# A graph network's prologue: the first block's rows gathered from x and normalised edge by edge

## The chip, the cores and the metric

The kernel runs on one core of one Trainium2 chip. The metric is the device time of one execution in microseconds; the kernel before took 6227.5 us, the median of three runs (6223.47, 6227.50 and 6228.35). A profile is one further execution of the same program under the hardware profiler; its own time is given beside it below.

The engines are named as the profile names them: PE (matrix products), DVE (vector engine), ACT (scalar engine), POOL (GpSimd), SP (the engine whose queue issues most transfers). Each engine works through its own instructions in order and waits for the others through semaphores.

## The reference

6250 nodes with 128 values each, 200000 edges sorted by their receiving node. Two layers, each added to x.

```python
h = jnp.maximum(_layernorm(x, axis=-1), 0.0)
x = x + L0(h, src, dst, W, attn_l, attn_r, bias)      # attention over edges
h = jnp.maximum(_layernorm(x, axis=-1), 0.0)
x = x + L1(h, edge_attr_4, edge_attr_8, ..., stack([src, dst]))

# L0
z = (feat @ W).reshape(N, HEADS, PER_HEAD)
el = jnp.einsum('nhp,hp->nh', z, attn_l)
er = jnp.einsum('nhp,hp->nh', z, attn_r)
e = jax.nn.leaky_relu(el[src] + er[dst], negative_slope=0.2)
a = jnp.exp(e - segment_max(e, dst)[dst])
out = segment_sum(z[src] * a[:, :, None], dst) / segment_sum(a, dst) + bias
```

Layer 1 runs a small network over each edge's attributes, multiplies the sender's row with its weights and sums the messages by receiver. For this change only the beginning matters: z and el of every node, er of every node, and the row (z, el) of the sender of every edge.

## The kernel before

The edges lie in 1563 tiles of 128 (one edge per partition), 16 tiles (KB) to a block: 98 blocks. A block's receivers fall into a window of nodes, so that sums over receivers are products with one-hot matrices on PE. Rows of senders are fetched from a table in DRAM: t0 (136 values: z and el) for layer 0, t1 and t1z (128 values) for layer 1.

*Prologue* (lines 842 to 957). The 50 tiles of x come in ten loads on SP's queue (line 865; the groups gx have 2, 3, 5, then 6 tiles, the last 4). Behind them on the same queue stand the index list src_col, the receivers twice (d_i, and q_i shifted by one edge) and a small off. A loop over k runs four stages of different groups side by side: statistics of group k on DVE (moments), the square root of group k-1 on ACT (deviation), the normalisation of group k-2, dealt out to ACT, POOL and DVE by tile number (lines 892 to 900), and for group k-3 the transposes and products on PE, with the ReLU (line 911) and the copies to zt on ACT, for the last two groups on DVE. zt goes to the table t0 on SP's queue; POOL copies its last eight columns to er_all. PE, DVE and ACT keep the order in which the code is written (manual_schedule); POOL and SP are ordered by the scheduler of the language.

Behind the loop POOL gathers the 16 tiles of block 0 from t0 into z_first (line 930). A gather is one indirect transfer of 128 rows, issued by POOL:

```python
nc.gpsimd.indirect_dma_start(
    out=to[:, k, :width], out_offset=None, in_=table,
    in_offset=bass.IndirectOffsetOnAxis(ap=src_col[:, t : t + 1], axis=0))
```

Meanwhile DVE tests whether the edges are as the fast path needs them (lines 932 to 950: is any receiver smaller than the one before, does a tile leave its window), writes the count to ok_i, and splits er_all into three bf16 parts er3 (lines 952 to 957). All engines read ok_i and branch (line 959) into even_edges.

*even_edges* (line 965). It opens the pools const, then z_pool (five row buffers of 16 x 136 values, tile g), then others; a pool takes the next free addresses, so that z_pool lies above the constants, which lie where the prologue's tiles were. SP loads the constants and, in the pool build, the receivers once more (d_i, q_i, nxt_i), from which DVE and ACT make masks. Then the loop of layer 0 over the blocks (line 1363): take_rows(g + 3) issues a later block's gathers on POOL, and the steps for blocks g-2 to g+2 are woven together on PE, DVE and ACT. One tile in every third block is fetched row by row on SP's queue instead (rows_by_row). Layer 1 (line 1488) has a loop of the same kind, with z_first used again for its first block.

Of the kernel before, what the change touches and what calls it, by code (L numbers as in the profile page):

```python
# [9 lines left out]
F32 = mybir.dt.float32  # L10
BF = mybir.dt.bfloat16
I32 = mybir.dt.int32
AF = mybir.ActivationFunctionType
OP = mybir.AluOpType
AX = mybir.AxisListType
# [3 lines left out]
P = 128  # L19
H = 8  # L20
D = 16
F = H * D
ZW = F + H
# [6 lines left out]
KB = 16  # L30
# [711 lines left out]
def tile_even_edges(  # L742
# [46 lines left out]
    def to_table(table, of, i, n, eng):  # L789

        if i == 0:
            eng.dma_start(table[: P - W0, :], of[W0:, 0, :])
            if n > 1:
                to = table[P - W0 : n * P - W0]
                eng.dma_start(to.rearrange("(j p) f -> p j f", p=P), of[:, 1:n, :])
            return
        to = table[i * P - W0 : (i + n) * P - W0]
        eng.dma_start(to.rearrange("(j p) f -> p j f", p=P), of[:, :n, :])
# [20 lines left out]
    def deviation(pool, mv, n, name, m=P):  # L819
        rs = pool.tile([P, n, 1], F32, name=f"rs{name}")  # L820
        nc.scalar.activation(rs[:m], mv[:m, :, 1:2], AF.Sqrt, bias=eps[:m])
        return rs

    def normal(pool, mv, rs, n, name, m=P):

        nc.vector.reciprocal(rs[:m], rs[:m])
        mr = pool.tile([P, n, 1], F32, name=f"mr{name}")
        nc.vector.scalar_tensor_tensor(mr[:m], mv[:m, :, 0:1], -1.0, rs[:m], op0=OP.mult, op1=OP.mult)
        return rs, mr
# [8 lines left out]
    def tiles_of(a, first):  # L838
        return a[first : first + TG * P * P].rearrange("(g t e) -> t g e", t=P, e=P)


    with tc.manual_schedule(engines={mybir.EngineType.PE, mybir.EngineType.DVE,
                                     mybir.EngineType.Activation}), \
# [11 lines left out]
        nc.scalar.sqrt(root, eps)  # L855
        w_ext = fx.tile([P, CW], F32, name="fw_ext")
# [9 lines left out]
        nc.sync.dma_start(src_col, srcc)  # L866
        d_i = fx.tile([P, TG, P], I32, name="fd_i")
        nc.sync.dma_start(d_i, tiles_of(dstt, P))
        q_i = fx.tile([P, TG, P], I32, name="fq_i")
        nc.sync.dma_start(q_i, tiles_of(dstt, P - 1))  # L870
        off = fx.tile([P, TG], F32, name="foff")
        nc.sync.dma_start(off, nums[:, NB * KB : NB * KB + TG])
# [7 lines left out]
        er_all = fx.tile([P, NX, H], F32, name="fer_all")  # L880
        NC = len(gx)
        mvs, rss, mrs, hs = {}, {}, {}, {}
        todo, done, outs = [], [], []
        for k in range(NC + 3):
            if 0 <= k - 1 < NC:
                rss[k - 1] = deviation(fp, mvs[k - 1], gx[k - 1][1], f"x{gx[k - 1][0]}")
            c = k - 2
            if 0 <= c < NC:
                i, n = gx[c]
                rs, mr = rss[c], mrs[c] = normal(fp, mvs[c], rss[c], n, f"x{i}")  # L890
                h = hs[c] = fp.tile([P, 10, P], F32, name="fh")
                for j in range(n):
                    by = (i + j) % 7
                    if by in ((2, 6) if c < NC - 2 else (2,)):
                        nc.scalar.activation(h[:, j, :], xs[c][:, j, :], AF.Identity,
                                             bias=mr[:, j, :], scale=rs[:, j, :])
                    else:
                        eng = nc.gpsimd if by in (0, 3, 5) and c < NC - 2 else nc.vector
                        eng.tensor_scalar(h[:, j, :], xs[c][:, j, :], mvs[c][:, j, 0:1],
                                          rs[:, j, :], op0=OP.subtract, op1=OP.mult)  # L900
            if k >= 3:
                i, n = gx[k - 3]
                zt = fp.tile([P, 10, CW], F32, name="zt")
                todo += [(k - 3, zt, j0, min(3, n - j0)) for j0 in range(0, n, 3)]
            while todo:
                c, zt, j0, m = todo.pop(0)
                p_t = fp_ps.tile([P, 4, P], F32, name="p_t")
                for j in range(m):
                    nc.tensor.transpose(p_t[:, j, :], hs[c][:, j0 + j, :], ident)
                h_t = fp.tile([P, 3, P], F32, name="h_t")  # L910
                nc.scalar.activation(h_t[:, :m], p_t[:, :m], AF.Relu)
                done.append((c, zt, j0, m, h_t))
                while len(done) > (1 if k < NC + 2 or todo else 0):
                    c, zt, j0, m, h_t = done.pop(0)
                    p_z = fp_ps.tile([P, 3, CW], F32, name="p_z")
                    for j in range(m):
                        nc.tensor.matmul(p_z[:, j, :], h_t[:, j, :], w_ext, start=True, stop=True)
                    outs.append((c, zt, j0, m, p_z))
                    while len(outs) > (1 if k < NC + 2 or todo or done else 0):
                        c, zt, j0, m, p_z = outs.pop(0)  # L920
                        copy = nc.scalar.copy if c < NC - 2 else nc.vector.tensor_copy
                        copy(zt[:, j0 : j0 + m, :], p_z[:, :m])
                        i, n = gx[c]
                        if j0 + m == n:
                            to_table(t0, zt[:, :, :ZW], i, n, nc.sync)
                            nc.gpsimd.tensor_copy(er_all[:, i : i + n, :], zt[:, :n, ZW:])
            if k < NC:
                i, n = gx[k]
                mvs[k] = moments(fp, xs[k], n, f"x{i}")
        gather(z_first, t0, range(KB), ZW)  # L930

        bad = fx.tile([P, TG, P], F32, name="fbad")
        nc.vector.tensor_tensor(bad, d_i, q_i, OP.is_lt)
        vs = fx.tile([P, 4], F32, name="fvs")
        nc.vector.tensor_reduce(vs[:, 0:1], bad.rearrange("p g e -> p (g e)"), AX.X, OP.add)
        w3 = fx.tile([P, 3, TG], F32, name="fw3")
        ef = fx.tile([P, 2, TG], F32, name="fef")
        nc.vector.tensor_sub(ef[:, 0, :], d_i[:, :, 0], off)
        nc.vector.tensor_sub(ef[:, 1, :], d_i[:, :, P - 1], off)
        nc.vector.tensor_single_scalar(w3[:, 0, :], ef[:, 0, :], 0.0, op=OP.is_lt)  # L940
        nc.vector.tensor_single_scalar(w3[:, 1, :], ef[:, 1, :], float(P), op=OP.is_ge)
        nc.vector.tensor_tensor(w3[:, 2, :], ef[:, 0, :], ef[:, 1, :], OP.is_equal)
        nc.vector.tensor_reduce(vs[:, 1:2], w3.rearrange("p a g -> p (a g)"), AX.X, OP.add)
        ones = fx.tile([P, 1], F32, name="fones")
        nc.vector.memset(ones, 1.0)
        p_v = fp_ps.tile([P, 4, P], F32, name="p_t")
        nc.tensor.matmul(p_v[:1, 0, :2], ones, vs[:, :2], start=True, stop=True)
        vr = fx.tile([1, 1], F32, name="fvr")
        nc.vector.tensor_reduce(vr, p_v[:1, 0, :2], AX.X, OP.add)
        nc.vector.tensor_copy(ok_i, vr)  # L950
# [14 lines left out]
def even_edges(tc, v):  # L965
# [5 lines left out]
    xp, dstc, y4, f8, bias, out, moments, deviation, normal, gather, tiles_of = (v[k] for k in (  # L971
        "xp", "dstc", "y4", "f8", "bias", "out", "moments", "deviation", "normal", "gather", "tiles_of"))
    with ExitStack() as ctx:
        const = ctx.enter_context(tc.tile_pool(name="fconst", bufs=1))
        z_pool = ctx.enter_context(tc.tile_pool(name="fz", bufs=5))
# [22 lines left out]
        wup = const.tile([P, P], F32, name="fwup")  # L998
        nc.sync.dma_start(wup, v["wup"])
        a1p = const.tile([P, KB // 2, P], F32, name="fa1p")  # L1000
        nc.sync.dma_start(a1p, v["a1p"])
        a2p = const.tile([P, P], F32, name="fa2p")
        nc.sync.dma_start(a2p, v["a2p"])
        a3p = const.tile([P, 2, P], F32, name="fa3p")
        nc.sync.dma_start(a3p, v["a3p"])
        b1 = const.tile([P, 1], F32, name="fb1")
        nc.sync.dma_start(b1, v["b1"])
        b2 = const.tile([P, 1], F32, name="fb2")
        nc.sync.dma_start(b2, v["b2"])
        wout = const.tile([P, 2, P], F32, name="fwout")  # L1010
        nc.sync.dma_start(wout, v["wout"])
# [11 lines left out]
        with tc.tile_pool(name="fbuild", bufs=1) as build:  # L1023
            d_c = build.tile([P, TU], I32, name="fd_c")
            nc.sync.dma_start(d_c, dstc)
            d_i = build.tile([P, TG, P], I32, name="fd_i")
            nc.sync.dma_start(d_i, tiles_of(dstt, P))
            q_i = build.tile([P, TG, P], I32, name="fq_i")
            nc.sync.dma_start(q_i, tiles_of(dstt, P - 1))
# [20 lines left out]
            nc.sync.dma_start(t1z[LATE * P - W0 :].rearrange("(j p) f -> p j f", p=P), zeros)  # L1050

# [796 lines left out]
```

## Time and profile before

| | |
|---|---|
| median of the runs | 6227.5 us |
| the profiled execution's own time | 3888.67 us |
| its span, first to last instruction | 3886.9 us |
| granted TensorE clock, mean | 0.803 |
| first gather of block 0 starts | 42.58 us |
| first gather of block 1 starts | 63.16 us |
| last gather starts | 3870.95 us |
| busy between 42.58 and 63.16: POOL, DVE, PE | 15.70, 5.34, 0.69 us |
| DMA share and GB/s, 0 to 42.58 us | 0.79, 220 |
| DMA share and GB/s, 63 to 1950 us | 0.28, 64 |

The profile is one execution; its durations are sums and means of that one. It was 2339 us shorter than the runs, and it holds nothing of the runs themselves. A line of a group gives: code line, engine, operation, output <- inputs by the program's names, count, then busy time, mean ns of one, idle time of the engine just before them and what ended most of it. "issue" is time in which the engine waited for nothing that the profile shows.

### The profile page before, as it was taken

To read this page: it belongs to the slowest core of one execution; us is meant where nothing else is said; L and a number is where in the kernel's file an instruction comes from. 1 tells how busy PE (TensorE), PEld (TensorE's weight loads), DVE (VectorE), ACT (ScalarE), POOL (GpSimd) and SP (SyncE) were. 2 spreads that over 40 slices of the span, in tenths; PEclk is the share of its full clock that TensorE was granted. 3 is DMA by queue.
4 is the path that set the end of the run, shared out by engine and by line. 5 is a ranking of instruction groups with operands and counts; after the bars stand their busy time and mean duration, and the time that the engine had idled before them with its cause. 6 is when DMAs were issued, how large, how long until landed. Compare 5 with 4: busy or idle time off the path is not lost. (4 is left out here: it accounts for less than half of the span.)

```text
span 3886.9 us, 62701 instructions
## 1 busy us (share of the span) xinstructions
PE 2848.8 (73%) x14785; PEld 2401.2 (62%) x14785; DVE 2224.5 (57%) x5408; ACT 1396.8 (36%) x3612; POOL 2913.0 (75%) x3096
## 2 busy tenths in 40 slices
PE   3766666666666766666678888888877777778777
PEld 3656656656556656666666666666666556656665
DVE  5544444444444444444457777677766666666666
ACT  3323232323322323232324444444444444444443
POOL 6777777777777777777777777777777777777776
PEclk6666666666666566666689999999999999999999
DMA  6222222222222222222222222222222222222221
GB/s 181 59 64 64 62 64 64 64 62 64 62 64 62 64 61 64 62 64 62 61 61 61 61 62 62 62 62 62 62 62 62 62 62 61 63 60 63 61 61 50
DMA packets 195262, 252.65 MB, mean 65 GB/s; under 512 B 78656, under 2 KB 145088, under 8 KB 194880
## 3 DMA queue, kind: packets, MB, share of 16 engines
q0 software_dynamic: 98048, 207.27, 22.6%
q1 hardware_dynamic: 96544, 41.19, 4.1%
q8 instruction: 120, 1.97, 0.2%
q14 instruction: 262, 2.15, 0.2%
q10 hardware_dynamic: 288, 0.07, 0.0%
HBM read 234.73 MB, written 13.25 MB: 64 GB/s over the span
## 5 line engine op out<-in xcount | busy, mean ns | idle before, releaser
L833 POOL DMA_INDIRECT g<-ft,fsrc x3024 | 2856.7, 945 | 922.4 <-issue 858.3
L1570 PE MATMUL p_u<-mj,s 128*128 128x256 f32 x3126 | 789.9, 397 | 217.9 <-DVE mj L1562 216.5
L1570 PEld LDWEIGHTS p_u<-mj,s 128*128 128x128 f32 x3126 | 588.9, 196 | 385.7 <-DVE mj L1562 310.9
L1234 PE MATMUL p_u<-g,s 128*128 128x136 f32 x3062 | 597.8, 376 | 0.4 <-DVE g L1229 0.4
L1234 PEld LDWEIGHTS p_u<-g,s 128*128 128x128 f32 x3062 | 572.1, 279 | 0.5 <-DVE g L1229 0.4
L1537 ACT ACTIVATE p_w<-p_w,yb 128x64 f32<-128x64 f32 x1563 | 450.3, 288 | 121.5 <-PE p_w L1533 80.4
L1553 DVE TENSOR_TENSOR vy<-g,p_i 128x384 f32<-128x384 f32 x387 | 212.9, 550 | 366.6 <-DMA g<-ft,fsrc 258.0
L1533 PE MATMUL p_w<-fa3p,h 128*128 128x256 f32 x1564 | 412.0, 387 | 0.0
L1151 PE MATMUL p_d<-fident,s 128*128 128x128 f32 x1563 | 384.7, 411 | 0.0
L1533 PEld LDWEIGHTS p_w<-fa3p,h 128*128 128x128 f32 x1564 | 289.4, 195 | 118.1 <-issue 52.5
L1176 DVE TENSOR_TENSOR e_s<-g,p_n 128x128 f32<-128x128 f32 x96 | 27.5, 286 | 578.6 <-DMA g<-ft,fsrc 566.2
L1518 ACT ACTIVATE h<-p_h,fb 128x512 f32<-128x512 f32 x196 | 134.6, 687 | 573.2 <-PE p_h L1516 571.8
L1151 PEld LDWEIGHTS p_d<-fident,s 128*128 128x128 f32 x1563 | 312.4, 225 | 37.6 <-issue 26.3
L1144 ACT COPY mk<-p_m 128x385 f32<-128x385 f32 (+1 forms) x99 | 47.6, 481 | 781.3 <-PE p_m L1141 781.2
L1229 DVE TENSOR_TENSOR g<-g,pe 128x1024 f32<-128x1024 f32 x193 | 225.5, 1209 | 129.2 <-ACT g L1220 126.4
L1153 ACT CAST d<-p_d 128x512 bf16<-128x512 f32 x391 | 228.8, 586 | 192.0 <-PE p_d L1151 141.6
L1179 PE MATMUL pe<-fident,e_s 128*128 128x128 f32 x98 | 39.1, 399 | 326.2 <-DVE e_s L1177 326.2
L1097 DVE TENSOR_TENSOR s<-p_n,fdloc 128x512 f32<-128x512 f32 x391 | 266.1, 682 | 6.7 <-ACT sv L1289 3.4
L1097 DVE TENSOR_TENSOR s<-p_i,fdloc 128x512 f32<-128x512 f32 x391 | 266.1, 681 | 3.8 <-ACT p_i L1512 3.8
L1516 PE MATMUL p_h<-ft,fa1p 128*128 128x128 f32 x1568 | 217.2, 283 | 63.3 <-DMA ft<-in_e_f_dram 63.1
L1516 PEld LDWEIGHTS p_h<-ft,fa1p 128*128 128x128 f32 x1568 | 210.6, 198 | 83.9 <-issue 65.3
L1523 ACT ACTIVATE h<-p_h,fb 128x512 f32<-128x512 f32 x196 | 134.7, 687 | 307.1 <-PE p_h L1520 307.1
(202 smaller groups left out, 3344.3 us busy)
## 6 DMA issues: line engine op xcount, KB each, us to landing
r<-ft SPq DMA_DIRECT2D x3968, 0.5 KB
r<-ft SPq DMA_DIRECT2D x3968, 0.5 KB
g<-ft,fsrc POOLq DMA_INDIRECT x3024
ft<-in_e_f_dram SPq DMA_DIRECT2D x98, 64.0 KB
yb<-in_e_y_dram SPq DMA_DIRECT2D x98, 32.0 KB
fx_all<-in_e_xp_dram SPq DMA_DIRECT2D x48, 64.0 KB
out_dram<-fx_all SPq DMA_DIRECT2D x47, 64.0 KB
ft<-sv SPq DMA_DIRECT2D x46, 64.0 KB
```

The costliest lines, as they stand in the source:

```text
L833: nc.gpsimd.indirect_dma_start(out=to[:, k, :width], out_offset=None, in_=table, in_offset=bass.IndirectOffsetOnAxis(ap=src_col[:, t : t + ...
L1097: nc.vector.tensor_tensor(s[:, :m], iota[:, None, :].to_broadcast([P, m, P]), dloc[:, t : t + m].unsqueeze(2).to_broadcast([P, m, P]), OP. ...
L1151: nc.tensor.transpose(p_d[:, k, :], c["s"][q][:, k, :], ident)
L1153: nc.scalar.copy(d[:, :m], p_d[:, :m])
L1229: nc.vector.tensor_mul(zh, zh, p_a[:, k0 : k0 + m].unsqueeze(3).to_broadcast([P, m, H, D]))
L1234: nc.tensor.matmul(c["p_u"][:, :ZW], c["s"][k // 4][:, k % 4, :], c["z"][:, k, :], start=c["o"] + k == 0, stop=c["o"] + k == KT[c["b"]] - 1)
L1516: nc.tensor.matmul(p_h[:, q, :], a1p[:, q0 + q, :], c["ft"], start=True, stop=True)
L1523: nc.scalar.activation(h2, p_h, AF.Silu, bias=b2)
L1533: nc.tensor.matmul(w[:, k : k + n].rearrange("p k a u -> p (k a u)"), c["h2"][q // 4][:, q % 4, :], a3p[:, :n].rearrange("p k f -> p (k f) ...
L1537: nc.scalar.activation(w[:, k, ::2, :], w[:, k, ::2, :], AF.Copy, scale=c["yb"][:, k0 + k, 0:1])
L1553: nc.vector.tensor_mul(vy, v_n, y_p)
L1570: nc.tensor.matmul(blk[b]["p_u"][:, :MW], u["s"][:, k, :], u["mj"][:, k, :], start=k0 + k == 0, stop=k0 + k == KT[b] - 1)
```

## The change

In the prologue, block 0's rows no longer come from t0. POOL gathers rows of x itself into z_first, straight behind its iota, with a short index list of its own (src_0, and row_0 = src_0 + 32). They are turned into (z, el) by the same code as the nodes (rows_of, called a second time with raw = "e"), in groups of 6, 6 and 4 tiles, behind all groups of nodes. Around it:

- POOL and SP keep the written order too. POOL normalises only five node tiles, all in the seventh and eighth group; the others go to DVE, as do the copies to er_all.
- zt has four buffers of 6 tiles instead of three of 10.
- d_i holds 129 receivers, so that q_i is not loaded; d_i and off are loaded behind the table write of the second group, src_col behind that of the fourth.
- the test of the edges (uneven_edges) stands ahead of the last copies to zt; its sum is taken by PE over bf16 flags (count_uneven), between the two passes.
- in even_edges z_pool is opened ahead of const, the loads of wup to wout stand behind the mask pool, and the receivers are loaded with 129 in a row here too.

```diff
+    def with_before(a):
+
+        t = tiles_of(a, P - 1)
+        return bass.AP(tensor=t.tensor, offset=t.offset,
+                       ap=[list(p) for p in t.ap[:-1]] + [[1, P + 1]])
...
     with tc.manual_schedule(engines={mybir.EngineType.PE, mybir.EngineType.DVE,
-                                     mybir.EngineType.Activation}), \
+                                     mybir.EngineType.Activation, mybir.EngineType.Pool,
+                                     mybir.EngineType.SP}), \
...
         nc.scalar.sqrt(root, eps)
+        src_0 = fx.tile([P, KB], I32, name="fsrc0")
+        nc.scalar.dma_start(src_0, srcc[:, :KB])
         w_ext = fx.tile([P, CW], F32, name="fw_ext")
         nc.scalar.dma_start(w_ext[:, :F], w0)
...
-        nc.sync.dma_start(src_col, srcc)
-        d_i = fx.tile([P, TG, P], I32, name="fd_i")
-        nc.sync.dma_start(d_i, tiles_of(dstt, P))
-        q_i = fx.tile([P, TG, P], I32, name="fq_i")
-        nc.sync.dma_start(q_i, tiles_of(dstt, P - 1))
+
+        d_i = fx.tile([P, TG, P + 1], I32, name="fd_i")
+        er_all = fx.tile([P, NX, H], F32, name="fer_all")
         off = fx.tile([P, TG], F32, name="foff")
-        nc.sync.dma_start(off, nums[:, NB * KB : NB * KB + TG])
+
+        def load(k):
+            if k == 1:
+                nc.sync.dma_start(off, nums[:, NB * KB : NB * KB + TG])
+                nc.sync.dma_start(d_i, with_before(dstt))
+            elif k == 3:
+                nc.sync.dma_start(src_col, srcc)
...
+        row_0 = fx.tile([P, KB], I32, name="frow0")
+        nc.vector.tensor_single_scalar(row_0, src_0, W0, op=OP.add)
+        for k in range(KB):
+            nc.gpsimd.indirect_dma_start(
+                out=z_first[:, k, :P], out_offset=None, in_=xp,
+                in_offset=bass.IndirectOffsetOnAxis(ap=row_0[:, k : k + 1], axis=0))
...
+        def uneven_edges():
+            nc.vector.tensor_tensor(bad, d_i[:, :, 1:], d_i[:, :, :P], OP.is_lt)
...
+            nc.vector.tensor_tensor(w3[:, 2, :], ef[:, 0, :], ef[:, 1, :], OP.is_equal)
+
+        def count_uneven():
+            p_v = fp_ps.tile([P, 512], F32, name="p_v", bufs=1)
+            b = bad.rearrange("p g e -> p (g e)")
+            for k in range(0, TG * P, 512):
+                n = min(512, TG * P - k)
+                nc.tensor.matmul(p_v[:1, :n], ones, b[:, k : k + n], start=k == 0, stop=False)
+            nc.tensor.matmul(p_v[:1, : 3 * TG], ones, w3.rearrange("p a g -> p (a g)"),
+                             start=False, stop=True)
+            vr = fx.tile([1, 1], F32, name="fvr")
+            nc.vector.tensor_reduce(vr, p_v[:1, :], AX.X, OP.add)
+            nc.vector.tensor_copy(ok_i, vr)
+
+        def rows_of(gx, xs, raw):
...
-                        eng = nc.gpsimd if by in (0, 3, 5) and c < NC - 2 else nc.vector
+                            late = by in (0, 3, 5) and NC - 4 <= c < NC - 2 and not raw
+                            eng = nc.gpsimd if late else nc.vector
...
+                if k == NC + 1 and not raw:
+                    uneven_edges()
+                for i, n, zt in ers:
+                    nc.vector.tensor_copy(er_all[:, i : i + n, :], zt[:, :n, ZW:])
+                ers = []
...
-                zt = fp.tile([P, 10, CW], F32, name="zt")
+                    zt = z_first[:, i : i + n, :] if raw else fp.tile([P, 6, CW], F32, name="zt", bufs=4)
...
-                        if j0 + m == n:
-                            to_table(t0, zt[:, :, :ZW], i, n, nc.sync)
-                            nc.gpsimd.tensor_copy(er_all[:, i : i + n, :], zt[:, :n, ZW:])
+                            if j0 + m == n and not raw:
+                                to_table(t0, zt[:, :, :ZW], i, n, nc.sync)
+                                ers.append((i, n, zt))
+                                load(c)
...
-        gather(z_first, t0, range(KB), ZW)
...
+        rows_of(gx, xs, "")
+        count_uneven()
+        gz = [(k, min(6, KB - k)) for k in range(0, KB, 6)]
+        rows_of(gz, [z_first[:, k : k + n, :P] for k, n in gz], "e")
...
     with ExitStack() as ctx:
+        z_pool = ctx.enter_context(tc.tile_pool(name="fz", bufs=5))
         const = ctx.enter_context(tc.tile_pool(name="fconst", bufs=1))
-        z_pool = ctx.enter_context(tc.tile_pool(name="fz", bufs=5))
...
-            d_i = build.tile([P, TG, P], I32, name="fd_i")
-            nc.sync.dma_start(d_i, tiles_of(dstt, P))
-            q_i = build.tile([P, TG, P], I32, name="fq_i")
-            nc.sync.dma_start(q_i, tiles_of(dstt, P - 1))
+            d_q = build.tile([P, TG, P + 1], I32, name="fd_q")
+            d_i, q_i = d_q[:, :, 1:], d_q[:, :, :P]
+            nc.sync.dma_start(d_q, with_before(dstt))
```

## The prediction

> **What bounds the kernel now.** I read the page first (busy shares, the costliest groups), then the chain of waits at the end, then POOL's waits summed by releaser, then the first 80 us in order of time on POOL, SP, DVE and ACT.
>
> ```profile
> span 3886.9 us, 62701 instructions
> ...
> PE 2848.8 (73%) x14785; PEld 2401.2 (62%) x14785; DVE 2224.5 (57%) x5408; ACT 1396.8 (36%) x3612; POOL 2913.0 (75%) x3096
> ...
> L833 POOL DMA_INDIRECT g<-ft,fsrc x3024 | 2856.7, 945 | 922.4 <-issue 858.3
> ```
>
> POOL's waits (releaser, us in total, times, longest), and the end of the chain of waits (start, us, what):
>
> ```profile
> POOL g L833 <- issue: 860.1, 2820, 0.3
> POOL g L833 <- PE p_u L1234: 18.6, 61, 0.3
> ```
>
> ```profile
> 3865.97 0.94 POOL g L833
> ...
> 3867.21 3.72 DMA g<-ft,fsrc
> ```
>
> POOL's 75% looks like slack. It is none: a row gather is 0.945 us of work and 0.30 us between one and the next, and no wait of POOL for a row buffer is longer than that 0.3 us. With the 40 gathers into fz_first and from ft1z there are 3064 (3024+16+16+8); the first starts at 42.58, the last at 3870.95, so 3828.4/3063 = 1.250 us each, from end to end. A chain of one kind of instruction, 98% of the span, sets the end. The other engines wait for its rows: from the fourth block on DVE's e_s of layer 0 idles 5 to 8 us for DMA g. So the end is (start of the stream) + (number of gathers) x 1.25 + a tail of 16 us behind the last one's start.
>
> The start in order of time, on POOL, then ACT, then DVE (start, us, engine, line, what; in brackets the idle time before it and who ended it):
>
> ```profile
> 38.86 1.80 POOL L926 COPY fer_all<-zt 128x32 f32<-128x32 f32 x1 [0.95 <-DVE zt L922]
> 42.58 1.17 POOL L833 DMA_INDIRECT fz_first<-ft,fsrc  x1 [1.92 <-issue]
> ...
> 61.91 0.95 POOL L833 DMA_INDIRECT fz_first<-ft,fsrc  x1 [0.30 <-DMA fz_first<-ft,fsrc]
> 63.16 0.94 POOL L833 DMA_INDIRECT g<-ft,fsrc  x1 [0.30 <-DMA fz_first<-ft,fsrc]
> ...
> 69.40 1.66 POOL L833 DMA_INDIRECT g<-ft,fsrc  x1 [0.30 <-issue]
> ```
>
> ```profile
> 23.92 0.52 ACT L922 COPY zt<-p_z 128x432 f32<-128x432 f32 x1 [4.35 <-DMA ft<-zt]
> ```
>
> ```profile
> 43.66 0.14 DVE L950 CAST fok<-fvr 1x1 int32<-1x1 f32 x1
> 43.73 0.34 DVE L953 CAST fer<-fer_all 128x400 bf16<-128x400 f32 x1
> ...
> 45.84 0.37 DVE L957 CAST fer<-frest 128x400 bf16<-128x400 f32 x1
> ```
>
> Here the reader sees the start: 16 gathers of block 0 from 42.58 to 63.16, then block 1's at once. DVE ended its part at 46.2, so the branch and the buffers were ready 17 us before POOL came to block 1. The change is worth what it takes off 63.16, and nothing else.
>
> **What the Trainium skill says.** Perfetto Trace Analysis, "DMA Instruction — SWDGE (GPSIMD)": the profiler ends such an instruction when the last descriptor is written, not when data has landed. The trace agrees: the chain has 3.72 us of DMA after a gather's end, and 0.94 is POOL's own work, whatever is read. DMA: Bandwidth & Descriptors, "Queues, rings and completion order": each DMA engine takes turns between its queue rows, packet by packet. So the new gathers share with the x loads and are not put behind them; no run shows such an overlap yet. SBUF — State Buffer, "SBUF: two separate sides": while DVE runs a two-port operation such as an fp32 SBUF copy, POOL can't write descriptors. Here, of the gathers between 43.7 and 46.5, beside DVE's er3 work, one took 1.32 and the others 0.94. So for the nine er_all copies that move to DVE beside the new gathers I charge nothing, and as a bound 9 x 0.4 us of POOL, which has nothing behind it there.
>
> **The change, part by part**, against the profiled execution's own 3888.67 us (span 3886.9).
>
> 1. *Sixteen gathers leave the stream.* 63.16 - 42.58 = 20.6 us of POOL. In their place POOL issues 16 gathers of x rows at the start: the index list lands on the ACT queue at about 3.3 us (the weights, first in that queue now, are used at 3.69), so they run from 3.7 to 3.7 + 16 x 1.25 + 0.2 = 24 us. Behind them wait POOL's five remaining normalisations. Before, the first of these started at about 20; DVE's input for them comes at about 25.5 (below), so at this pace nobody waits.
>
> 2. *The node pass.* ACT's 4.35 us wait for a table write (and DVE's 3.26 for ACT behind it) goes: a fourth zt buffer, q_i no longer loaded, d_i and src_col sent between table writes. Added to DVE: 12 normalisations taken from POOL (17 before, 5 after) x 0.27 (five took 1.37) = 3.2, and nine er_all copies, no row for DVE, 0.1 to 0.2 each, taken as 1.2 together. DVE's last statistics end at 27.6; 27.6 - 3.3 + 3.2 + 1.2 = 28.7. From the last deviation (31.66) to the last zt copy (38.80) it was 7.1, so the node pass ends at about 36 instead of 38.8. The comparison of dst (1.88 + 0.7) moves ahead of the last zt copies, where DVE idled 2.60 for PE; should d_i land late, it adds up to 2.6.
>
> 3. *ok.* Two sums on DVE (1.89, 0.19) become five matmuls, none like them in the trace: the nearest, 128x385 bf16, takes 0.48, so 0.5 to 2.2 us behind the last node matmul; I take 1.2. Then a reduction of 512 (as 128x512: 0.68) and the cast (0.14): ok stands at about 38.
>
> 4. *The edge pass*, all of it behind ok on DVE: 16 statistics (six took 1.64: 4.4), three reciprocals with their companion (0.32: 1.0), 14 normalisations (3.8), the tail through PE and ACT to the last copy (5.4 in the node pass, with more copies on ACT; I take 4.0), then er3 (43.73 to 46.2: 2.5). Sum 15.7, bounds 13.5 to 17.5.
>
> 5. *What block 1 waits for.* The rows' buffers now lie on the x tiles, which are read early, but the built instruction list shows the first gather behind the branch waiting for all four other queues, and for the DVE count that the last er3 cast reaches: the tiles of the prologue's pool are released together. So an early ok buys nothing, and POOL stands idle from about 30 to 38 + 15.7 + 0.3 = 54.0. In the kernel before the same wait was met at 46.2. Behind this gather is the whole stream.
>
> 6. *SP.* Its constants wait for the second pool of the prologue, to about 51 instead of 46.4; one of two 1664-run loads (2.94 us of SP and more in its queue) and seven constants leave the path to the masks, so these come at about 76 instead of 81. By-row transfers start at about 68 to 73 (70.9 before). Neither is near: block 1's buffer was free at 127.7, and POOL wants it again after 80 gathers, 54 + 100 = 154.
>
> Sum: 63.16 - 54.0 = 9.2 us sooner, bounds 5 to 13. Profiled: 3888.7 - 9.2 = 3879.5.
>
> **To the runs' median.** It is 6227.5, 2339 us above the profiled execution; the profile doesn't show where those are. Three readings: they lie off this path: 9 us gained. They lie in the gathers: (2339 + 3828)/3063 = 2.01 each; block 1 then starts at 42.6 + 16 x 2.01 + 0.6 = 75.4 before; after, POOL is busy with x rows until 36, its normalisations end at 38.6 where PE needs them, and from there 7.4 + 17.6 lead to about 64: 11 gained. Everything is slower by 1.6: 15 gained. I take the middle, 11: 6216.5 us. Two tenths of a percent, 12.5 us, is about what a measurement of this kernel tells from no change; the forecast lies just inside.
>
> **Rivals.**
> - *The stream starts at ok, not at the end of the pass* (0.15): POOL's first gather at 39 to 46, 17 to 24 us sooner, 17 to 38 in the median: 6200. For it: ok is early and the buffers' old contents are dead by 25 us. Against it: the listed wait.
> - *The median isn't set by the gathers' start* (0.13): if the 2339 us sit in another chain, such as SP's 7936 by-row transfers (0.39 us each here, 80% of the span), which starts as before, nothing moves: 6227. Against it: in the profile SP is never what POOL or DVE waits for.
> - *Slower: x rows are gathered when the DMA engines are full* (0.10). In the first 42.6 us they are 79% busy at 220 GB/s. Four gathers from 69.4 on, while SP's loads were landing, took 1.39 to 1.66 instead of 0.94. A gather also waits for the landing of the eighth before it. POOL's five normalisations stand behind all 16, PE and the rest of both passes behind those: block 1 starts at 3.7 + 16 x (pace of an x-row gather) + 2.8 + 7.4 + 17.6 = 31.5 + 16 x pace, once the pace is above 1.4. Break-even with 63.16 is 1.98 us; at 1.66 + 0.30 next to nothing is gained. Slower by 12.5 us needs 1.5 us above the stream's own pace, so 2.75 in the profile; the median would be 6243.
>
> **How the numbers follow.** The case worked out has 0.60, with 6 to 16 us gained; 0.20 of this lies beyond 12.5 us (everything slower by 1.6, or the upper bounds of steps 2 to 4). Faster by over 0.2%: 0.20 + 0.15 = 0.35. Slower: 0.10 and 0.02 for a pace changed by the buffers' place (fz_first, at a low address, is filled at the same 0.94 as g, so little). Same: 0.40 + 0.13 = 0.53. Range: 6198 takes in most of the first rival, 6234 the second and the milder part of the third.
>
> **What would show it.** x-row gathers from about 4 to 24 us; no wait of ACT for a table write; ok at about 38; POOL idle, then the first g at 54; 1.25 us per gather and the tail unchanged; span 3878. Wrong if the first g is before 47 (the wait is not what I read) or after 60 (x rows or edge pass mis-sized), or if the span falls by 9 and the median by far more or nothing.

## The result, and the profile after

| | median of 12 runs, us | lowest to highest |
|---|---|---|
| before | 6229.37 | 6218.53 to 6251.77 |
| after | 6227.84 | 6209.67 to 6246.74 |

The ratio is 1.0 with a 95% interval of 0.9987 to 1.0013: no difference that can be measured, where the prediction named 11 us (0.18%) as the likeliest gain. The profiled execution of after took 6234.45 us. The profile of before that the prediction is argued from took 3888.67 us, a kind of execution that no run here showed again; so a new profile of the unchanged kernel before (e1 below, 6230.78 us) is what the profile of after is compared with.

The page of after: the span, the busy shares, the gathers.

```profile
span 6232.7 us, 62862 instructions
...
PE 3023.0 (49%) x14836; PEld 2511.7 (40%) x14836; DVE 2233.8 (36%) x5485; ACT 1391.7 (22%) x3625; POOL 2899.4 (47%) x3074
...
L833 POOL DMA_INDIRECT g<-ft,fsrc x3024 | 2857.0, 945 | 3225.0 <-issue 1558.5
```

And the same group in the usual execution of before (e1):

```profile
L833 POOL DMA_INDIRECT g<-ft,fsrc x3024 | 2855.9, 944 | 3197.1 <-issue 1522.4
```

One gather still takes 0.945 us, and DVE and ACT have the same busy time as in the 3889 us execution (2224.5 and 1396.8 there). What has grown is POOL's idle time ahead of gathers: 3225 us, where it was 922. So of the prediction's three readings of the missing 2339 us, two are out at once: the gathers are not 2.01 us each, and the work is not 1.6 times slower. POOL's waits in after (releaser, us in total, times, longest) say what the idle time is:

```profile
POOL g L833 <- issue: 1560.9, 2897, 19.2
POOL g L833 <- DVE mj L1608: 840.9, 62, 68.0
POOL g L833 <- PE p_d L1197: 441.8, 28, 19.0
```

Most of these are waits of up to 68 us for the blocks that still use the five row buffers, where in the 3889 us execution POOL waited no longer than 0.3 us ahead of a gather of g. The stream of gathers runs in bursts of 15 or 16, one for each block, and stops in between. So the missing time lies in stops within the stream itself, and the reading that is left, time off this path, does not hold as stated.

The start in order of time, POOL in after (start, us, line, what; in brackets the idle time before it and who ended it):

```profile
3.67 1.09 POOL L899 DMA_INDIRECT fz_first<-in_e_xp_dram,frow  x1 [2.60 <-DVE stx L814]
...
22.55 0.94 POOL L899 DMA_INDIRECT fz_first<-in_e_xp_dram,frow  x1 [0.30 <-issue]
...
37.39 1.65 POOL L951 TENSOR_SCALAR fh<-fxs,mvx,rsx 128x128 f32<-128x128 f32 x2 [0.60 <-issue]
67.12 1.03 POOL L833 DMA_INDIRECT g<-ft,fsrc  x1 [28.08 <-DMA fbias_b<-in_e_bias_dram]
```

and in e1, the kernel before:

```profile
42.62 1.17 POOL L833 DMA_INDIRECT fz_first<-ft,fsrc  x1 [1.92 <-issue]
...
63.18 0.94 POOL L833 DMA_INDIRECT g<-ft,fsrc  x1 [0.30 <-issue]
```

The x rows are gathered from 3.67 to 23.5 us, as forecast to half a microsecond. Yet block 1's first gather comes at 67.1, not at 54.0; the kernel before has it at 63.2 in both kinds of execution. The change moved the start of the stream 3.9 us back. (The view names a DMA of a constant at the end of POOL's wait; the last er3 cast, below, ends at 66.16, and POOL's queue moves on at once.) DVE in after shows where the time went:

```profile
13.74 0.48 DVE L814 BATCH_NORM_STATS2 stx<-fxs 128x6 f32<-128x128 f32 x2
15.05 0.18 DVE L816 BATCH_NORM_AGGREGATE mvx<-stx 128x2 f32<-128x6 f32 x1 [0.83 <-DVE stx L814]
15.15 0.26 DVE L814 BATCH_NORM_STATS2 stx<-fxs 128x6 f32<-128x128 f32 x1
16.45 0.18 DVE L816 BATCH_NORM_AGGREGATE mvx<-stx 128x2 f32<-128x6 f32 x1 [1.04 <-issue]
...
24.86 0.17 DVE L828 SCALAR_TENSOR_TENSOR mrx<-mvx,rsx 128x6 f32<-128x6 f32 x1 [1.87 <-remote]
...
48.39 0.14 DVE L928 CAST fok<-fvr 1x1 int32<-1x1 f32 x1
...
65.79 0.37 DVE L1002 CAST fer<-frest 128x400 bf16<-128x400 f32 x1
```

Between 13.7 and 24.9 us the node pass's statistics crawl: one pair of instructions in 1.4 us, once 2.1, with waits for DVE's own last result or for nothing that the profile shows, where a pair took 0.26. At 24.9, a moment after POOL's last x-row gather ended at 23.5, the pace is normal again. ok stands at 48.53 (forecast: 38), and the last er3 cast ends at 66.16.

### The profile page after: what moved, and what is told of

Same layout as the page of the kernel before. It is cut to its first block, busy times and chain, and to the rows that moved or that the text cites. A ratio compares the mean times of both kernels' runs of the same rounds, so it can differ in the third digit from the quotient of the medians.

```text
span 6232.7 us, 62862 instructions
## 1 busy us (share of the span) xinstructions
PE 3023.0 (49%) x14836; PEld 2511.7 (40%) x14836; DVE 2233.8 (36%) x5485; ACT 1391.7 (22%) x3625; POOL 2899.4 (47%) x3074
## 5 line engine op out<-in xcount | busy, mean ns | idle before, releaser
L1616 PE MATMUL p_u<-mj,s 128*128 128x256 f32 x3126 | 931.2, 450 | 672.9 <-DVE mj L1608 588.2
L1616 PEld LDWEIGHTS p_u<-mj,s 128*128 128x128 f32 x3126 | 683.1, 226 | 858.8 <-DVE mj L1608 643.0
L1601 DVE TENSOR_TENSOR p_w<-g,p_w 128x128 f32<-128x128 f32 x387 | 112.9, 292 | 1159.9 <-ACT p_w L1583 1034.5
L1208 PEld LDWEIGHTS <-d 128*128 128x128 bf16 x1563 | 99.3, 113 | 878.4 <-ACT d L1199 562.8
L1627 PE MATMUL p_n<-fwout,m_t 128*128 128x128 f32 x192 | 57.6, 454 | 548.6 <-ACT m_t L1625 534.3
L1197 PE MATMUL p_d<-fident,s 128*128 128x128 f32 x1563 | 321.5, 358 | 0.0
L1566 PE MATMUL p_h<-h,fa2p 128*128 128x512 f32 x392 | 250.6, 727 | 144.5 <-ACT h L1564 89.5
L1214 DVE TENSOR_REDUCE p_n<-p_er 128x128 f32<-128x384 f32 (+1 forms) x97 | 54.6, 563 | 651.0 <-PE p_u L1280 231.4
L1208 PE MATMUL p_er<-fer,d 128*128 128x24 bf16 x784 | 55.1, 185 | 463.1 <-ACT d L1199 260.2
L1197 PEld LDWEIGHTS p_d<-fident,s 128*128 128x128 f32 x1563 | 260.0, 193 | 25.0 <-DVE feq L1074 16.0
```

The costliest lines, as they stand in the source:

```text
L1197: nc.tensor.transpose(p_d[:, k, :], c["s"][q][:, k, :], ident)
L1566: nc.tensor.matmul(p_h.rearrange("p q e -> p (q e)"), a2p, c["h1"].rearrange("p q e -> p (q e)"), start=True, stop=True)
L1616: nc.tensor.matmul(blk[b]["p_u"][:, :MW], u["s"][:, k, :], u["mj"][:, k, :], start=k0 + k == 0, stop=k0 + k == KT[b] - 1)
```

## The experiments

Times are compared with the kernel before on the same chip: 6239.0 us for e1 to e4, 6297.9 us for e5 to e8 and, on a third chip, for e9 to e12. e1, e4, e6, e7, e8 and e11 are single executions.

**e1: the kernel before, unchanged.** For a profile of the usual execution.

> The kernel before, unchanged, for a profile of an execution that takes the usual time. Theory S (in the usual executions SyncE's row-by-row transfers set the time): about 6230 us, SyncE puts out one row every 0.75 us as in the profile of the kernel after (0.46 in the profiled execution of 3889 us), and the gathers on GpSimd keep 0.945 us each, with stalls of 5 to 45 us at block ends where no row buffer is free. Theory G (the gathers are slower, 2.01 us each): about 6230 us, a gather every 2.0 us without such stalls. Theory A (everything is 1.6 times slower): the mean durations of matmuls and gathers are 1.6 times those of the 3889 us profile. It also shows whether the prologue of the kernel before is as late as that of the kernel after in such an execution: first gather of block 1 at about 63 us if not, 75 or more if so.

6230.78 us. A gather takes 0.944 us, and the busy times of DVE, ACT and POOL are those of the 3889 us execution (PE's is 6% longer), so theories G and A fall. The prologue is as early as in that execution (first g at 63.18), so the late node pass belongs to the change. SP's row transfers by tile (count; shortest, median, longest ns; first and last start), in the 3889 us execution of before, then in after. MOVE is the work on a register that stands ahead of each row, DMA_DIRECT2D issues the transfer:

```profile
L1078 SPq MOVE r<-ft x7936: 29/29/38, 70.9 to 3709.5; - x199
L1078 SPq DMA_DIRECT2D r<-ft x7936: 227/228/384, 70.9 to 3709.6; - x199
```

```profile
L1124 SPq MOVE r<-ft x7936: 1/29/1404, 83.3 to 6035.3; - x199
L1124 SPq DMA_DIRECT2D r<-ft x7936: 1/228/1425, 83.4 to 6035.3; - x199
```

(3709.6 - 70.9)/7935 = 0.46 us a row there, (6035.3 - 83.4)/7935 = 0.75 us in after, and 0.75 in e1. (The prediction's 0.39 is the pace within one run of 152 rows.) The medians are equal; some instructions take 0.7 or 1.4 us. From the starts of the rows in the trace of after: about 1.0 us from one row to the next while POOL gathers, 0.48 in its pauses. SP was thus busy with rows throughout, which seemed to speak for theory S.

**e2, e3: no row transfers**, in the kernel after and in the kernel before.

```diff
-        by_row = [b for b in range(3, NB - 2) if b % 3 == 0]
+        by_row = []
```

> The kernel after with no block fetched row by row: the 62 tiles that SyncE fetched in 7936 row transfers become 62 more gathers on GpSimd (3126 in place of 3064). Theory S: SyncE's stream is gone and the gathers are the bound, 67 us + 3126 x 1.25 us + 16 us = about 3990 us, 0.64 of the time before, in all runs. Theory G: 44 + 3126 x 2.01 + 16 = about 6343 us, 2% slower. Theory A: 3990 x 1.6 = about 6380 us, slower by 2.4%.

> The kernel before with no block fetched row by row, the pair of e2. Theory S: also about 3990 us; as the gathers are then the bound from start to end, the change is worth what it moves the first gather of block 1: 9 us in the prediction (e2 shorter by 0.23%), -4 us if the times of the two profiles held (63.2 against 67.1 us). Theory G: 6350 us. Theory A: 6390 us.

e2: 5454.26 us, ratio 0.8742 (0.8730 to 0.8754). e3: 5449.36 us, ratio 0.8738 (0.8726 to 0.8750). All three theories missed: the rows cost 785 us, but without them the time is still 1460 us above what the gathers alone would take. Between the two, after is 4.9 us longer, with its first g 2.3 us later (65.4 against 63.1); the intervals overlap. e3 is the fastest version of the study and beats both kernels by an eighth.

**e4: one block in four by rows**, in the kernel after.

```diff
-        by_row = [b for b in range(3, NB - 2) if b % 3 == 0]
+        by_row = [b for b in range(3, NB - 2) if b % 4 == 0]
...
-            while rows_until.n < (block + 3) * P / 12 and next(rows, 0) is None:
+            while rows_until.n < (block + 3) * P / 16 and next(rows, 0) is None:
```

> The kernel after with one block in four fetched row by row in place of one in three (23 blocks for 31, 5888 row transfers for 7936, 16 gathers more), the rows handed out at three quarters of the pace. Theory S: 83 + 5888 x 0.75 + 197 = about 4700 us. Theory G: 16 gathers more at 2.01 us, about 6265 us. Theory A: about 6260 us.

5851.45 us: between the numbers of the theories, and half way from e2 to after. Theory S as stated, an SP stream at a fixed pace that alone sets the end, is wrong.

What the traces of e1, e2 and after share is that everything but POOL gets on slowly while POOL gathers. That became theory H: while GpSimd gathers, the other engines are held up. The next four take the kernel of e2 as their base, so that rows don't blur them.

**e5: the x-row gathers behind the node pass.**

```diff
-        for k in range(KB):
-            nc.gpsimd.indirect_dma_start(
-                out=z_first[:, k, :P], out_offset=None, in_=xp,
-                in_offset=bass.IndirectOffsetOnAxis(ap=row_0[:, k : k + 1], axis=0))
...
         rows_of(gx, xs, "")
         count_uneven()
+        for k in range(KB):
+            nc.gpsimd.indirect_dma_start(
+                out=z_first[:, k, :P], out_offset=None, in_=xp,
+                in_offset=bass.IndirectOffsetOnAxis(ap=row_0[:, k : k + 1], axis=0))
```

> The kernel after without row transfers (e2), with the 16 gathers of x rows issued behind the node pass and not beside it. Theory H (while GpSimd gathers, the other engines are held up): the node pass is back at the pace of the kernel before, its first table store at 15 to 20 us (24.0 in e2) and its last store issued by 39 us (46.6 in e2); the gathers then run from about 39 to 59 us, the edge pass behind them, and the first gather of block 1 comes at about 74 us (65.4 in e2). Rival P (the node pass is late because of its new order or its full DMA engines, not because of gathers): the last store stays at 46 us. Time: the 9 us of later start are given back at the first stops of the gather stream, so within 6 us of e2 (5454 us).

**e6: e5, with 16 computing instructions on POOL in the gathers' old place.**

```diff
+        aside = fx.tile([P, KB, P], F32, name="faside")
+        for k in range(KB):
+            nc.gpsimd.tensor_scalar(aside[:, k, :], jp, 1.0, 2.0, op0=OP.subtract, op1=OP.mult)
```

> e5 with 16 computing instructions on GpSimd (128x128 subtract and multiply into a tile that nobody reads, about 0.86 us each) where the kernel after has its 16 gathers. Theory H: GpSimd being busy is not what holds the others, the gathers are: node pass as in e5, last store by 39 us. Rival P: a busy GpSimd is enough, last store at about 46 us as in e2.

**e7: e5, with 16 gathers of one word per row in that place.**

```diff
+        aside = fx.tile([P, KB, 1], F32, name="faside")
+        for k in range(KB):
+            nc.gpsimd.indirect_dma_start(
+                out=aside[:, k, :], out_offset=None, in_=xp.rearrange("r (f o) -> (r f) o", o=1),
+                in_offset=bass.IndirectOffsetOnAxis(ap=row_0[:, k : k + 1], axis=0))
```

> e5 with 16 gathers of one 4-byte word per row (into a tile that nobody reads) where the kernel after has its 16 gathers of 512-byte rows. If the bytes that the gathers move hold the others up: node pass as in e5, last store by 39 us. If issuing a gather does, whatever its width: last store at about 46 us as in e2, with a gather every 1.25 us.

The table of windows from 12 to 24 us (length, then busy us and instructions of PE, PEld, DVE, ACT, POOL; granted clock, DMA share, GB/s), for after, e5, e6, e7 and e1 in this order:

```profile
12.00:24.00 12.00, 3.33 (x12) 2.30 (x11) 3.46 (x19) 1.55 (x4) 8.75 (x10) 1.00 0.48 124
```

```profile
12.00:24.00 12.00, 11.15 (x63) 9.70 (x62) 11.86 (x77) 8.97 (x25) 0.64 (x1) 1.00 0.66 182
```

```profile
12.00:24.00 12.00, 10.47 (x63) 8.95 (x62) 11.86 (x77) 8.95 (x25) 0.70 (x1) 1.00 0.67 178
```

```profile
12.00:24.00 12.00, 3.40 (x11) 2.37 (x11) 3.46 (x19) 1.55 (x4) 8.74 (x10) 1.00 0.26 54
```

```profile
12.00:24.00 12.00, 8.42 (x52) 7.87 (x52) 9.64 (x65) 6.14 (x17) 9.44 (x14) 0.94 1.08 301
```

In these 12 us DVE ran 77 instructions where POOL did not gather, and 19 where it did, with whole rows or with single words alike (54 GB/s moved in e7, 124 in after: the bytes are not it). A POOL that computes doesn't do it: in e1 it is busy for 9.44 of the 12 us with normalisations and DVE runs 65 instructions. e6's own POOL work took 0.62 us each and was over at 11.1, ahead of this window. So here is the window from 4 to 11 us, for e5, where POOL did nothing, and for e6, where it computed throughout:

```profile
4.00:11.00 7.00, 3.31 (x12) 2.57 (x12) 5.53 (x38) 1.84 (x7) 0.00 (x0) 1.00 1.11 289
```

```profile
4.00:11.00 7.00, 3.33 (x12) 2.56 (x12) 5.66 (x38) 1.88 (x7) 7.00 (x12) 1.00 1.15 294
```

DVE ran 38 instructions in both (31 in after, 34 in e7). The node pass follows. First table store and first count matmul behind the node pass:

| | first table store | count matmul |
|---|---|---|
| e2, 16 gathers beside it | 24.01 | 45.55 |
| e5, none before 27.8 us | 15.24 | 38.88 |
| e6, POOL computing | 15.19 | 38.84 |
| e7, 16 one-word gathers | 27.72 | 51.36 |

(e7 also has its 16 gathers of whole rows from 40.2 us on, ahead of its count matmul.)

The last square root of the node pass, in after and then in e5, whose first gather starts at 27.76:

```profile
39.81 0.37 ACT L821 ACTIVATE rsx<-mvx,feps 128x4 f32<-128x4 f32 x1
```

```profile
28.34 0.32 ACT L821 ACTIVATE rsx<-mvx,feps 128x4 f32<-128x4 f32 x1
```

Theory H holds here, rival P falls. Two things were off in e5: POOL came to the gathers at 27.8 and not at 39, so they ran beside the second half of the node pass after all (ok at 45.3, last table store 42), and the first g was at 66.2 and not at 74. Its time, 5526.51 us or a ratio of 0.8774 (0.8758 to 0.8789), stands beside the kernel before on another chip. By ratio it is 0.3% above e2, where one kernel on two chips (e3 and e12) differs by 0.1%; with a first g only 0.8 us later than in e2 this is not explained.

**e8: four gathers more for each block**, 779 in all, into a tile that nobody reads.

```diff
+        more = ctx.enter_context(tc.tile_pool(name="fmore", bufs=3))
...
         def gathered(table, tiles, width):
+            gather(more.tile([P, 4, ZW], F32, name="more"), table, list(tiles)[:4], width)
             return gather(z_pool.tile([P, KB, ZW], F32, name="g"), table, tiles, width)
```

> e2 with the first four tiles of each block gathered a second time into a tile that nobody reads, some 780 gathers more, 4 x 1.25 = 5.0 us of GpSimd for each block. GpSimd stands idle about 7.5 us for each block in e2. Theory H: each gather holds the other engines up for half of its time or more, so the blocks take longer by 2.5 to 5 us each, 5940 to 6430 us in all. Rival I (the blocks wait for something that gathers don't touch, and GpSimd's idle time takes the new gathers): 5454 us as e2.

6534.01 us, 1007.5 more than e5 on the same chip: 1.29 us for each added gather, more than its own 1.25 and above the range given for H. (e8 has e2's early x rows; with e2's ratio carried to this chip the cost is 1.32.) POOL's idle time took none of it: without the 0.30 us behind each gather it is about 1620 us in e5 and 1670 in e8. How the others are held is seen in ACT's waits of e2 and of e8:

```profile
ACT h_t L1325 <- remote: 614.4, 44, 14.2
```

```profile
ACT h_t L1327 <- remote: 826.1, 44, 25.1
```

The view knows no releaser for these 44 waits, which are 14.0 us long on average in e2 and 18.8 us in e8. They last until about the end of the burst of gathers beside them: of those over 8 us in e8, the 16 beside a burst of 16 gathers took 13.6 us on average, and the 27 beside one of 23 or 24 took 22.4. ACT waits for a transposition on PE. One case of e2, in order of time, with the last gather of the burst:

```profile
488.54 0.27 PE L1323 MATMUL p_n<-fident,xn 128*128 128x128 f32 x1
497.71 0.94 POOL L833 DMA_INDIRECT g<-ft,fsrc  x1 [0.30 <-issue]
501.56 0.28 ACT L1325 ACTIVATE h_t<-p_n 128x128 f32<-128x128 f32 x1 [14.06 <-remote]
503.30 0.77 PE L1330 MATMUL p_n<-fwup,h_t 128*128 128x128 f32 x2 [14.50 <-DVE s L1143]
```

PE ends the transposition at 488.81 and then stands idle, yet in the trace's record PE's semaphore still counts on, at 492.4, 493.1, 495.9, 498.7 and 501.5, and ACT starts at 501.56. In the 44 cases ACT starts 12.3 us on average after the end of the transposition, as a rule 3.0 us after the end of the last gather; in the 3889 us execution it started 0.04 us after it in all 49 cases. So what comes late here is not the work but the signal that it is done. Late signals are not the whole of the hold: SP's MOVE waits for no semaphore and is stretched too. What delays them, no run shows.

**e9, e10: the stream starts later**, by 24 one-word gathers ahead of block 0's, in the kernel before (e9) and in e3's (e10); e12 is e3 again, as the pair of e10.

```diff
+        aside = fx.tile([P, 24, 1], F32, name="faside")
+        gather(aside, t0.rearrange("r (f o) -> (r f) o", o=1), range(24), 1)
         gather(z_first, t0, range(KB), ZW)
```

> The kernel before (row transfers kept) with 24 gathers of one 4-byte word per row, into a tile that nobody reads, ahead of block 0's gathers: the gather stream proper starts 24 x 1.25 = 30 us later (first gather of block 1 at about 93 us, 63.2 in e1). Theory of the prediction (the stream of gathers is the bound from its start to the end): 30 us longer than the kernel before, ratio 1.0048. Theory S (SyncE's row transfers, held up while gathers run, set the end, and a later start of the gathers is taken up at the stream's first stops): within 8 us of the kernel before, ratio 0.9987 to 1.0013.

> The same 24 gathers ahead of block 0's in the kernel before without row transfers (the pair is e12). Where SyncE no longer sets the end, each gather costs its whole time as in e8, and the start counts: 25 to 35 us longer than e12, about 0.5%. If the first stops take it up here too: within 5 us of e12.

> e3 once more, as the pair of e10 on the same chip: 0.874 of the time before.

POOL in e9:

```profile
93.01 0.94 POOL L833 DMA_INDIRECT g<-ft,fsrc  x1 [0.30 <-issue]
```

The first g is 29.8 us later than in e1, and e9 takes 6333.59 us, 35.7 us longer than the kernel before, ratio 1.0057 (1.0041 to 1.0072). e10 takes 5536.2 us and e12 5511.02 (ratios 0.8788, 0.8772 to 0.8804, and 0.8747, 0.8730 to 0.8764): 25.2 us. So I was wrong to write, in the expectations of e5 and e9, that the first stops take a late start up. I had it from e1 and after, whose streams are level by gather 112 (242.5 and 242.4 us); a few us either way between two single executions prove nothing. Stops or not, the start of the stream goes on to the end about one for one, as the prediction had it. One thing is left open: the 24 gathers hold the other engines too while they run, and at e8's price of 1.29 us each they would cost 31 us, so the two pairs don't tell a later start from added gathers.

**e11: the rows from fixed addresses**, in the kernel before.

```diff
-                    if e % 32 == 0:
-                        _, offs = nc.values_load_multi_w_load_instructions(
...
                     nc.sync.dma_start(to[e : e + 1, :].bitcast(mybir.dt.uint8),
-                                      flat[ds(offs[e % 32], size)].unsqueeze(0))
+                                      flat[(b * P + e) % 6000 * size : ((b * P + e) % 6000 + 1) * size].unsqueeze(0))
```

> The kernel before with the same 7936 row transfers of the same sizes to the same tiles, but from fixed addresses: no row numbers are read into registers, so SyncE has one instruction for each row in place of two and no register loads; the rows fetched are not those of the graph. Theory S (SyncE's instructions are held up and set the end): SyncE has less than half of its work, and the time falls to that of the kernel without rows or near it, 5400 to 5650 us. If the transfers themselves, or the copies on ScalarE that follow them, cost the 785 us between e2 and the kernel before: 6150 us or more.

6047.49 us, 250 less than the kernel before: neither of the two. SP's waits for other engines show that it no longer sets the end; the same two groups come to 100.9 and 51.4 us in e1:

```profile
SPq L1585 <- DVE fx_all L1577: 1067.2, 46, 31.7
SPq L1293 <- ACT sv L1284: 432.1, 30, 53.3
```

So of the 787 us that the rows cost on this chip (6297.9 - 5511.0), SP's register work, with the scattered addresses, is 250. Where the other 536 lie was not settled.

## Why the prediction was right, and where not

The measured time lies in its range, and no measurable change was its likeliest class (0.53). Its main case, 9.2 us sooner in the profile and 11 in the median, did not come. That the range holds the result is luck as far as this case goes: it was wide enough for a loss of 4 us as well as for a gain of 9.

1. *The gathers leave the stream, and the x rows take 3.7 to 24 us*: right, 3.67 to 23.5. The third rival, slower x-row gathers, did not occur: 1.26 us from one to the next, the first ones while the DMA engines were full. But "at this pace nobody waits" priced only the queue behind the gathers on POOL. What they do to the engines beside them was the cost, and it had no term in the sum.
2. *The node pass*: the stall of 4.35 us for a table write is gone, as said. ok came at 48.5 instead of 38 (steps 2 and 3), 10.5 us late. The hold accounts for it. The last square root of the node pass stands at 39.81 in after and at 28.34 in e5 (lines above). The prediction's sum puts it at about 28.7, so the sum was right for a node pass without gathers beside it. From there to the last table copy it took 7.7 us in after (7.1 in the prediction), and 13.4 in e5, where the gathers run beside this part.
3. *The edge pass*: 48.5 to 66.2, 17.6 us for 15.7, just past the upper bound. Its tail through PE and ACT and back, from the last normalisation at 57.3 to the last copy at 63.9, took 6.5 where I had taken 4.0.
4. *What block 1 waits for*: right. POOL stood idle from 39.0, long past ok, until the last er3 cast, then 0.96 us (0.3 taken). 10.5 + 1.9 + 0.7 = 13.1 is all of the way from 54.0 to 67.1.
5. *SP*: rows from 83.4 us, not 68 to 73, since the same lateness stands ahead of them.
6. *The start goes to the end one for one*: right in effect as far as e9 and e10 tell (36 and 25 us for 30), wrong in its reason for the usual execution, where POOL stops for buffers in every block.

So the step that failed is the second: the node pass was costed as if gathers beside it were free, and they delayed its last square root by 11 us. With 3.9 us of later start in place of 9.2 us of earlier, and one for one, after should be about 4 us slower, 0.06%: too little to see. The rival whose number came true, 6227 because SP's row transfers set the median, was right in the number and not in its cause, as far as e9 tells: 24 gathers ahead of the stream moved the median by 36 us with the row transfers in place.

## What to carry to other kernels

Before moving gathers on GpSimd beside other work, count the instructions that the other engines complete in the same window with and without them; a free GpSimd and free DMA engines do not make them free. Where one profiled execution and the runs differ by a third, take another profile before arguing from it. Price a fetch by what it does to the whole: here row transfers that look cheap on an idle queue cost an eighth of the time, and dropping them is worth far more than the change under study.

## What the hardware showed that was not expected

- While GpSimd issued gathers, DVE ran 19 instructions in 12 us in place of 77, and SP put out a row in about 1.0 us in place of 0.48; one-word gathers did the same to DVE, computing on GpSimd did not. In 44 waits of e2 the signal of a finished matmul reached ACT 12.3 us late on average, where it took 0.04 us without the hold. The Trainium skill (SBUF — State Buffer, "SBUF: two separate sides") says that on the engine side only the port pair shared by GpSimd and DVE causes contention. That does not cover what is seen here: SP is held too, and a GpSimd that computes for 9.44 of 12 us leaves DVE its pace. What delays the signals stays open.
- In the one execution of 3889 us gathers ran without a break and SP's rows took 0.46 us: the hold was absent. What decides between the two was not found.
- Each added gather cost 1.29 us of the whole time (e8) with GpSimd idle for 43% of it, 18% being the 0.30 us behind each gather.
